# What layers 2 and 3 make of the context alone, moved into the first six steps of layer 0 and kept in DRAM

## The chip, the cores and the metric

The kernel runs on one core of one Trainium2 chip. TensorE (PE) multiplies, VectorE (DVE), ScalarE (ACT) and GpSimd (POOL) work on what it leaves in PSUM and on SBUF, and SyncE (SP) only issues DMAs. Every engine takes its instructions in the order of the program and waits on semaphores for the others. Time is the device time of one launch in microseconds; a comparison goes by the median of several runs.

## The reference, cut to what matters

Four layers follow each other on `x` (4 batches, 1024 rows, 256 features); each also reads the same context `ctx` (4 batches, 77 rows, 256 features), with 16 heads.

```
x = L0(x, ctx)   # causal self-attention joined with the context's keys, then a feed-forward net
x = L1(x, ctx)   # Taylor-feature attention on the context, and a window of 64 on x itself
# L2: cross-attention, heads of 16
q = x @ Wq.T + bq;  k = ctx @ Wk.T + bk;  v = ctx @ Wv.T + bv
p = softmax(where(mask, -inf, (q k^T / 4) * fside))
x = layernorm(x + (p v) @ Wo.T + bo)
# L3: cross-attention, heads of 64
n = rmsnorm(x)
p = softmax((n @ wq) (ctx @ wk)^T)
x = x + (p (ctx @ wv)) @ wo
```

In layers 2 and 3, `k`, `v`, every product of `v` with its head's rows of `Wo` or `wo`, and in layer 3 the product of `k` with its head's rows of `wq`, depend on the context and the weights alone, not on `x`.

## The kernel before, in words

**Layer 0 and layer 1.** Each batch is worked in four *quads* of four heads. A step of layer 0 (`step`, L449) takes the maxima of one quad (`Max0`: scores on PE, `tensor_reduce` into `mpart` on DVE, L565) paired with the weights of the quad before (`Sum0`: scores again, `exp` on ACT, L630, then the product with the values). Both write pairs of PSUM banks out of a pool of two (`big`). After each such burst comes a gap (`gap`, L419), where jobs are advanced: a `Job(gen, n, a, b)` (L400) is to have made n of its steps in proportion to the share of the step that has passed between a and b. What the jobs make is filler for PE: projections of the next quad, statistics, the feed-forward net of the batch before (`ffn`, L764). All fillers share a PSUM pool of three banks, `sm`. Step (b, quad) = (0, 0) has no weights beside the maxima. The order within an engine is the order in which the program is written out; nothing is reordered later.

**Layers 2 and 3** work tile by tile (128 rows of `x`, 32 tiles) in *slots* (`slot2` L1217, `slot3` L1362), software-pipelined over three or four tiles, with jobs in two gaps of each slot. `jobs2` and `jobs3` (L1569, L1581) give the jobs of a batch. What depends on the context alone is made for one batch during the batch before:

- In layer 2, `prep2(b)` (L1176) makes the values and keys (`apart2`, L1131: `pk` on PE, bias on DVE, one copy for each of four heads with the others masked, on POOL), then `U` = each head's values times its rows of `Wo` (`folded_values`, L1153), then the features and the queries of the batch. For batch 0 it runs alone, between the layers (L1551).
- `folded_values` makes 16 heads in 8 steps; a step has two matmuls (`pu`), an eviction on ACT and one on DVE (`us`, four buffers) and about three DMAs that put the 77 rows of each head where `U` wants them: `U` is a list of 16 x 77 = 1232 rows in chunks of 128.
- In layer 3, `folded3(b)` (L1320) makes the keys (`pk`), `G` = keys times `wq` (`pg`), the values (`pk`) and `U`. A slot then multiplies `x`'s features with `G` (`ps<-G,xT`) and the softmax with `U` (`po<-U,pT`).

**Queues.** All DMAs are issued by SP, in the order of the program: at the start the loads, then for each quad the spreading of its queries and keys to their rows (`spread`, L331; a stage buffer `st` to `qk`), in layer 2 two loads for each tile (`load_sides`, L1209), in layer 3 the output.

**SBUF.** The weights live in slots with tags: `s3` holds `w1`, later layer 2's weights; `s4` holds `w2`, later layer 3's `wq`; `s7` holds layer 1's `wout`; `hT` (3 buffers) and `y` belong to the feed-forward net. `first.close()` (L1544) gives the memory of layers 0 and 1 to the pool `late`.

Of the kernel before, what the change touches and what calls it, by code (L numbers as in the profile page):

```python
# [31 lines left out]
def tile_xattn_seq(ctx: ExitStack, tc: tile.TileContext, d: dict, out: bass.AP):  # L32
# [123 lines left out]
    for b in range(1, NB):  # L156
        load_x(b)
    ctn = work.tile([S, NB - 1, D], F32, name="ctn", tag="hT", bufs=3)
    nc.sync.dma_start(out=ctn, in_=d["ctx_1024"][1:NB].rearrange("b s e -> s b e"))

    def other_contexts():
# [8 lines left out]
    w1 = wpool.tile([P, 2, FF], F32, name="w1", tag="s3")  # L170
    load_plain(w1, d["L0_xattn_w1"])
    w2 = wpool.tile([P, 8, D], F32, name="w2", tag="s4")
    load_plain(w2, d["L0_xattn_w2"])
    load_cols_of(
        ("L0_xattn_gf", 2), ("L0_xattn_bf", 2), ("L0_xattn_b1", 8), ("L1_xattn_norm_w", 2),
        ("L2_xattn_bq", 2), ("L2_xattn_bk", 2), ("L2_xattn_bv", 2), ("L3_xattn_norm_w", 2),
# [7 lines left out]
    hsel = cpool.tile([P, HH], F32, name="hsel")  # L184
# [23 lines left out]

    def later_constants():
# [18 lines left out]

        nc.gpsimd.memset(hsel, 1.0)
        nc.gpsimd.affine_select(  # L230
            out=hsel, in_=hsel, compare_op=ALU.is_ge, fill=0.0, base=0,
            pattern=[[-DH, HH]], channel_multiplier=1,
        )
        nc.gpsimd.affine_select(
            out=hsel, in_=hsel, compare_op=ALU.is_ge, fill=0.0, base=DH - 1,
            pattern=[[DH, HH]], channel_multiplier=-1,
        )
# [526 lines left out]
    def ffn(b):  # L764
# [5 lines left out]
        for q in range(5):  # L770
            for half in range(2):
                if q < 4:
                    h = hs[q, half] = work.tile([P, 4, D], F32, name="hT", tag="hT", bufs=3)
                    for f in range(4):
                        ph = sm.tile([P, D], F32, name="ph", tag="sm")
                        fs = slice(P * (4 * half + f), P * (4 * half + f + 1))
                        for c in range(2):
                            mm(
                                ph, w1[:, c, fs], yT[:, c, D * q : D * q + D],
                                start=(c == 0), stop=(c == 1),  # L780
                            )
# [8 lines left out]
                if q and half == 0:  # L790
                    h2 = [hs.pop((q - 1, k)) for k in range(2)]
                    for i in range(2):
                        po = sm.tile([P, D], F32, name="po", tag="sm")
                        for f in range(8):
                            mm(
                                po, h2[f // 4][:, f % 4, P * i : P * i + P], w2[:, f, :],
                                start=(f == 0), stop=(f == 7),
                            )
# [6 lines left out]

    l1 = {}
    l1["wout"] = wpool.tile([P, 4, D], F32, name="wout", tag="s7")
    load_plain(l1["wout"], d["L1_xattn_Wout"])
# [306 lines left out]
    l2 = {}  # L1115

    def load2():
        w = wpool.tile([P, 4, 2, D], F32, name="w2s", tag="s3")
        for i, key in enumerate(("L2_Wq_t", "L2_Wk_t", "L2_Wv_t", "L2_Wo_t")):
            l2[key[3:5]] = w[:, i]  # L1120
            load_plain(w[:, i], d[key])
# [4 lines left out]
    def consts2():  # L1126

        l2["hsel"] = late.tile([P, 4], F32, name="hsel4", tag="hsel4", bufs=1)
        nc.gpsimd.tensor_tensor(l2["hsel"], hsel[:, 0:4], hsel[:, 4:8], ALU.add)

    def apart2(b, w, bias):  # L1131


        pk = sm.tile([P, 2, S], F32, name="pk2", tag="sm")
        for o in range(2):
            for c in range(2):
                mm(
                    pk[:, o, :], w[:, c, P * o : P * o + P], ctxT[:, b, c, :],
                    start=(c == 0), stop=(c == 1),
                )  # L1140
        kp = late.tile([P, 2, S], F32, name="kp", tag="kp", bufs=1)
        kb = late.tile([P, 2, 4, S], F32, name="kb", tag="kb", bufs=3)
        for o in range(2):
            nc.vector.tensor_scalar(
                kp[:, o, :], pk[:, o, :], bias[:, o : o + 1], None, ALU.add
            )
            nc.gpsimd.tensor_tensor(
                kb[:, o], kp[:, o, :].unsqueeze(1).to_broadcast([P, 4, S]),
                l2["hsel"].unsqueeze(2).to_broadcast([P, 4, S]), ALU.mult,
            )  # L1150
        return kb

    def folded_values(U, lhs_of, rhs_of, head_of):  # L1153


        for f in range(8):
            us = late.tile([P, 2, D], F32, name="us", tag="us", bufs=4)
            pu = [sm.tile([P, D], F32, name="pu", tag="sm") for _ in range(2)]
            for e in range(2):
                mm(pu[e][:S], lhs_of(f, e), rhs_of(f, e), skip_group_check=True)  # L1160
            nc.scalar.copy(us[:S, 0, :], pu[0][:S])
            nc.vector.tensor_copy(us[:S, 1, :], pu[1][:S])
            for e in range(2):
                at = S * head_of(f, e)
                done = 0
                while done < S:
                    c, p0 = divmod(at + done, P)
                    n = min(P - p0, S - done)
                    nc.sync.dma_start(out=U[p0 : p0 + n, c, :], in_=us[done : done + n, e, :])
                    done += n  # L1170
            yield
# [4 lines left out]
    def prep2(b):  # L1176

        x = xs[b]
        vb = apart2(b, l2["Wv"], cols["L2_xattn_bv"])
        yield  # L1180
        kb = apart2(b, l2["Wk"], cols["L2_xattn_bk"])
        yield
        U = late.tile([P, NC, D], F32, name="U2", tag="qu")

        yield from folded_values(
            U, lambda f, e: vb[half_rows(e), f // 4, f % 4, :],
            lambda f, e: l2["Wo"][half_rows(e), f // 4, :],
# [5 lines left out]
        for o in range(2):  # L1193
            for q in range(2):
# [10 lines left out]
                if o and q:  # L1205
                    shared["b2", b] = (qT, kb, U)
# [416 lines left out]
```

## Time and profile before

| what | value |
|---|---|
| median of 3 runs | 2560.67 us (2560.18 to 2564.87) |
| the profiled execution, its own time | 2567.04 us |
| its span, first to last instruction | 2565.3 us |
| mean granted TensorE clock | 0.965 |
| busy: PE, PE weight loads | 2351.2 us (92%), 1432.8 us (56%) |
| busy: DVE, ACT, POOL | 1444.1 us (56%), 1025.3 us (40%), 605.5 us (24%) |
| layer 0's first step begins | 41.2 us |
| layers 0 and 1 end | about 1825 us |
| layer 2's slots | about 1850 to 2194 us |
| layer 3's slots | about 2190 to 2562 us |

A row of the windows view has the stretch, its length, the busy time and the number of instructions for PE, PEld, DVE, ACT and POOL, the granted TensorE clock, the share of the DMA engines and GB/s. A row of the groups view has the line, engine, operation, tiles out<-in, shapes, the number of instructions, then busy time and mean duration of one in ns, then the idle time of that engine just before them. One fp32 matmul stands as two records on PE, and matmuls overlap: busy time divided by the count is what one record costs in a stream, the mean is its latency. L45 is the helper that issues nearly all matmuls, so groups are told apart by their tiles.

### The profile page before, as it was taken

To read this page: it belongs to the slowest core of one execution; us is meant where nothing else is said; L and a number is where in the kernel's file an instruction comes from. 1 tells how busy PE (TensorE), PEld (TensorE's weight loads), DVE (VectorE), ACT (ScalarE), POOL (GpSimd) and SP (SyncE) were. 2 spreads that over 40 slices of the span, in tenths; PEclk is the share of its full clock that TensorE was granted. 3 is DMA by queue.
4 is the path that set the end of the run, shared out by engine and by line. 5 is a ranking of instruction groups with operands and counts; after the bars stand their busy time and mean duration, and the time that the engine had idled before them with its cause. 6 is when DMAs were issued, how large, how long until landed. Compare 5 with 4: busy or idle time off the path is not lost.

```text
span 2565.3 us, 40942 instructions
## 1 busy us (share of the span) xinstructions
PE 2351.2 (92%) x16658; PEld 1432.8 (56%) x16658; DVE 1444.1 (56%) x2429; ACT 1025.3 (40%) x1700; POOL 605.5 (24%) x867
## 2 busy tenths in 40 slices
PE   5888788989989898999999999999798998999999
PEld 3333333444444443445567666666476776777877
DVE  4645566544664446542644444444388898675554
ACT  1234343433433443444334434345365655232222
POOL 2011131111301113101422323333133333212212
PEclk8899998999999999999899999999899999999999
DMA  5000000000000001000100211011232321001000
GB/s 152 14 14 5 14 6 14 6 14 2 5 14 6 14 6 34 1 9 10 18 7 12 57 18 18 15 17 39 74 119 85 104 75 58 14 23 31 15 29 17
DMA packets 55631, 75.86 MB, mean 30 GB/s; under 512 B 14823, under 2 KB 46483, under 8 KB 55443
## 3 DMA queue, kind: packets, MB, share of 16 engines
q1 hardware_dynamic: 55442, 73.24, 11.2%
q8 instruction: 132, 2.16, 0.4%
q14 instruction: 57, 0.46, 0.1%
HBM read 41.30 MB, written 4.19 MB: 18 GB/s over the span
## 4 chain that ended last, share of the span: by engine, by line
PE 75%; DVE 14%; ACT 5%; issue 3%; DMA 1%; POOL 1%; SPq 1%; DVEq 0%; ACTq 0%; POOLq 0%
PE ps L45 32%; PE po L45 15%; DVE mpart L565 6%; PE pp L45 5%; PE pv L45 5%; PE ph L45 4%; ACT pe L630 2%; PE psT L1106 2%; PE ppv L45 2%; PE pvw L45 2%; PE pk L45 2%; PE pu L45 1%; PE pvl L45 1%; PE ptx L302 1%; PE pt L506 1%
## 5 line engine op out<-in xcount | busy, mean ns | idle before, releaser
L45 PE MATMUL ps<-qk 32*128 32x192 f32 (+8 forms) x5760 | 631.4, 473 | 130.4 <-DVE mpart L565 69.9
L630 ACT ACTIVATE pe<-ps 128x1024 f32<-128x1024 f32 (+2 forms) x384 | 363.2, 952 | 673.0 <-PE ps L45 667.1
L565 DVE TENSOR_REDUCE mpart<-ps 128x2 f32<-128x1024 f32 (+3 forms) x448 | 409.3, 933 | 361.6 <-PE ps L45 360.7
L45 PEld LDWEIGHTS ps<-qk 32*128 32x128 f32 (+1 forms) x5760 | 295.5, 187 | 420.6 <-DVE mpart L565 166.3
L45 PE MATMUL po<-U,pT 128*128 128x256 f32 (+1 forms) x1280 | 295.3, 386 | 3.2 <-DVE x L1270 2.9
L45 PEld LDWEIGHTS po<-U,pT 128*128 128x128 f32 (+1 forms) x1280 | 242.0, 193 | 48.3 <-issue 12.7
L633 POOL TENSOR_SCALAR_AFFINE_SELECT pe<-pe 128x256 f32<-128x256 f32 (+1 forms) x192 | 94.8, 494 | 613.7 <-ACT pe L630 602.4
L877 DVE TENSOR_REDUCE mrow<-ps 128x4 f32<-128x768 f32 x128 | 122.6, 958 | 144.7 <-PE ps L45 144.3
L1107 ACT COPY pT<-psT 128x512 f32<-128x512 f32 (+1 forms) x192 | 92.8, 519 | 248.9 <-PE psT L1106 248.5
L952 ACT ACTIVATE pew<-ps 128x768 f32<-128x768 f32 x128 | 103.5, 812 | 175.2 <-PE ps L45 174.4
L957 POOL TENSOR_SCALAR_AFFINE_SELECT pew<-pew 128x512 f32<-128x512 f32 x128 | 81.3, 635 | 349.2 <-ACT pew L952 349.0
L45 PE MATMUL pv<-pe,va 128*32 128x512 f32 (+3 forms) x1536 | 163.6, 514 | 0.1
L45 PE MATMUL ps<-G,xT 128*128 128x308 f32 x512 | 143.0, 423 | 0.0
L1401 POOL TENSOR_TENSOR s<-s,den 128x1232 f32<-128x1232 f32 x32 | 71.9, 2248 | 278.9 <-DVE den L1400 268.5
L45 PE MATMUL ph<-yT,w 128*128 128x256 f32 x512 | 136.0, 400 | 0.9 <-DVE qk L491 0.9
L1232 ACT ACTIVATE s<-s,nm 128x77 f32<-128x77 f32 x512 | 131.2, 348 | 11.3 <-DVE nm L1264 11.3
L45 PEld LDWEIGHTS ph<-yT,w 128*128 128x128 f32 x512 | 92.4, 195 | 50.9 <-issue 37.7
L45 PE MATMUL po<-w,hT 128*128 128x256 f32 x512 | 118.0, 384 | 0.0
L1106 PE MATMUL psT<-ident,s 128*128 128x128 f32 x640 | 93.9, 277 | 24.0 <-POOL s L1278 9.7
L45 PEld LDWEIGHTS po<-w,hT 128*128 128x128 f32 x512 | 96.1, 191 | 21.7 <-issue 9.5
L45 PEld LDWEIGHTS ps<-G,xT 128*128 128x128 f32 x512 | 92.5, 190 | 26.9
L491 DVE TENSOR_TENSOR qk<-pm,qk 128x512 f32<-128x512 f32 x64 | 44.1, 689 | 106.4 <-PE pm L489 106.4
(180 smaller groups left out, 3246.9 us busy)
## 6 DMA issues: line engine op xcount, KB each, us to landing
side<-in_fside_t SPq DMA_DIRECT2D x32, 616.0 KB
qk<-st SPq DMA_DIRECT2D x256, 64.0 KB
side<-in_mask_t SPq DMA_DIRECT2D x32, 154.0 KB
U<-us SPq DMA_DIRECT2D x56, 77.0 KB
x<-in_x SPq DMA_DIRECT2D x8, 512.0 KB
out<-x SPq DMA_DIRECT2D x32, 128.0 KB
w<-in_L_xattn_w SPq DMA_DIRECT2D x2, 1024.0 KB
qk<-kc SPq DMA_DIRECT2D x64, 4.8 KB
```

The lines of the kernel that those rows point to most:

```text
L45: nc.tensor.matmul(o, lhsT, rhs, start=start, stop=stop, **kw)
L491: nc.vector.tensor_tensor(qs, pm.rearrange("p i n -> p (i n)"), qs, ALU.add)
L565: nc.vector.tensor_reduce(mpart[bl][:, i, 2 * p : 2 * p + 2, ci], ps[:, :, o : o + w], axis=AX.X, op=ALU.max,)
L630: nc.scalar.activation(pp[:n, :, o:512], ps[:n, :, o:512], AF.Exp, scale=SC)
L633: nc.gpsimd.affine_select(out=own, in_=own, compare_op=ALU.is_ge, fill=0.0, base=0, pattern=[[0, 2], [0, k], [1, P]], channel_multiplier=-1,)
L877: nc.vector.tensor_reduce(mo, ps.rearrange("p j (i n) -> p j i n", i=2)[:, :, :, 0 : P + WIN], axis=AX.X, op=ALU.max, negate=True,)
L952: nc.scalar.activation(pp[:, :, :, 0 : P + WIN], ps.rearrange("p j (i n) -> p j i n", i=2)[:, :, :, 0 : P + WIN], AF.Exp, scale=SC,)
L957: nc.gpsimd.affine_select(out=pf[:, :, 0:P], in_=pf[:, :, 0:P], compare_op=ALU.is_ge, fill=0.0, base=0, pattern=[[0, 4], [1, P]], channel_ ...
L1106: nc.tensor.transpose(ps[:, k, :], s[:, P * c : P * c + P], ident)
L1107: nc.scalar.copy(pT[:, 4 * group : 4 * group + n, :], ps[:, 0:n, :])
L1232: nc.scalar.activation(hs, hs, AF.Exp, bias=p1["nm"][:, h : h + 1], scale=SC)
L1401: nc.gpsimd.tensor_tensor(s3, s3, den.unsqueeze(2).to_broadcast([P, H, S]), ALU.mult)
```

## The change

For all four batches at once (4 x 77 = 308 columns, `NS`), layer 0's first six steps make what layers 2 and 3 need of the context: in step (0, 0) layer 2's values (`values2`), `U` (`folded2`) and keys (`keys2`), in (0, 1) layer 3's keys (`heads3("wk")`), in (0, 2) its `G` (`keys3`), in (0, 3) its values (`heads3("wv")`), in (1, 0) and (1, 1) its `U` (`folded3`). The finished tiles go through one staging tile `stg` of 1024 columns, in which `place(n, size)` hands out n regions in turn, and are written to DRAM (`kept_k`, `kept_u`, `kept_g`). `folded` takes 128 of the 308 rows at a time, whatever batch they are of, so a head needs three matmuls where it needed four. Layer 2's keys come back in one load for all batches, `U` and `G` by batch, at 0.4 of the batch before; `G` comes in runs of 77 values.

The weights for this are loaded at the start, in `s3`, `s4` and `y`; the feed-forward net's `w1` and `w2`, and `wout`, come later, when these slots are free. The masks of heads are made ahead of layer 0 (`head_masks`, which POOL and DVE run behind the first constants), and the contexts of batches 1 to 3 are turned at the start of step (0, 0). `apart2`, `folded_values`, `consts2` and the old `folded3` are gone.

```diff
     ctn = work.tile([S, NB - 1, D], F32, name="ctn", tag="hT", bufs=3)
     nc.sync.dma_start(out=ctn, in_=d["ctx_1024"][1:NB].rearrange("b s e -> s b e"))
+    load_cols_of(("L2_xattn_bv", 2), ("L2_xattn_bk", 2))
+    l2 = {}
+    w2s = wpool.tile([P, 3, 2, D], F32, name="w2s", tag="s3")
+    for i, key in enumerate(("L2_Wv_t", "L2_Wo_t", "L2_Wk_t")):
+        l2[key[3:5]] = w2s[:, i]
+        load_plain(w2s[:, i], d[key])
+    load_x(1)
+    l3 = {}
+    def load3(key, pool, tag, **kw):
+        l3[key] = pool.tile([P, 2 if key in ("wk", "wv") else 8, 1024 if key in ("wk", "wv") else D],
+                            F32, name="l3" + key, tag=tag, **kw)
+        load_plain(l3[key], d["L3_" + key])
...
+    load3("wk", wpool, "s4")
+    for b in range(2, NB):
+        load_x(b)
+    load3("wq", work, "y", bufs=1)
...
+    def head_masks():
...
+        nc.vector.tensor_reduce(
+            hsel2, hsel.rearrange("p (r e) -> p e r", e=2), axis=AX.X, op=ALU.add
+        )
+        nc.vector.tensor_reduce(
+            hsel4, hsel.rearrange("p (g e) -> p e g", e=4), axis=AX.X, op=ALU.add
+        )
...
+    NS = NB * S
+    dram = ctx.enter_context(tc.tile_pool(name="dram", bufs=1, space=bass.MemoryType.DRAM))
+    kept_k = dram.tile([P, 2, 4, NS], F32, name="kept_k")
+    kept_g = dram.tile([P, 2, 8, 2, NS], F32, name="kept_g")
+    kept_u = [dram.tile([NB, H, S, D], F32, name=f"kept_u{i}") for i in range(2)]
+    stg = wpool.tile([P, 1024], F32, name="stg", tag="s7")
+    turn = [0]
...
+    def place(n, size):
+        turn[0] += 1
+        o = 1024 // n * (turn[0] % n)
+        return stg[:, o : o + size]
...
+    def of_contexts(w, o):
+        pk = sm.tile([P, NB, S], F32, name="pk", tag="sm")
+        for c in range(2):
+            mm(pk, w[:, c, P * o : P * o + P], ctxT[:, :, c, :], start=(c == 0), stop=(c == 1))
+        return pk.rearrange("p b s -> p (b s)")
+    def values2():
+        vb = shared["v2"] = []
+        for o in range(2):
+            pk = of_contexts(l2["Wv"], o)
+            v = work.tile([P, 2, NS], F32, name="v2", tag="hT", bufs=3)
+            for e in range(2):
+                nc.vector.tensor_scalar(
+                    v[:, e, :], pk, cols["L2_xattn_bv"][:, o : o + 1], hsel2[:, e : e + 1],
+                    ALU.add, ALU.mult,
+                )
+            vb.append(v)
+            yield
...
+    def keys2():
+        for o in range(2):
+            pk = of_contexts(l2["Wk"], o)
+            for e in range(4):
+                k = place(3, NS)
+                nc.vector.tensor_scalar(
+                    k, pk, cols["L2_xattn_bk"][:, o : o + 1], hsel4[:, e : e + 1],
+                    ALU.add, ALU.mult,
+                )
+                nc.sync.dma_start(out=kept_k[:, o, e, :], in_=k)
+                if e % 2:
+                    yield
...
+    def folded(dst, pairs, act):
+        for heads, lhs, rhs in pairs:
+            for at, lo in ((0, 0), (P, P), (NS - P, 2 * P)):
+                hi = at + P
+                us = place(2, 512).rearrange("p (e n) -> p e n", e=2)
+                pu = [sm.tile([P, D], F32, name="pu", tag="sm") for _ in range(2)]
+                for e in range(2):
+                    mm(pu[e], lhs[e][:, at:hi], rhs[e], skip_group_check=True)
+                for e in range(2):
+                    evict(us[:, e, :], pu[e], act or e == 0)
+                b = lo // S
+                while lo < hi:
+                    n = min(hi, S * b + S) - lo
+                    nc.sync.dma_start(
+                        out=dst[b, heads, lo - S * b : lo - S * b + n, :].rearrange("e s n -> s e n"),
+                        in_=us[lo - at : lo - at + n],
+                    )
+                    lo, b = lo + n, b + 1
+                yield
...
+    def folded2():
...
+                for e in range(2):
+                    h = HH * o + 2 * r + e
+                    two = [slice(HP * (r + k), HP * (r + k) + HP) for k in range(2)]
+                    pairs.append((
+                        slice(h, h + 3, 2), [shared["v2"][o][q, e, :] for q in two],
+                        [l2["Wo"][q, o, :] for q in two],
+                    ))
...
+    def heads3(key):
+        kv = shared[key] = [
+            work.tile([P, 3, NS], F32, name="kv3", tag="hT", bufs=3) for _ in range(3)
+        ]
+        for f in range(8):
+            evict(kv[f // 3][:, f % 3, :], of_contexts(l3[key], f), f % 2)
+            yield
...
+    def keys3():
+        for f in range(8):
+            for c in range(2):
+                pg = [sm.tile([P, NS], F32, name="pg", tag="sm") for _ in range(2)]
+                for e in range(2):
+                    r = slice(64 * e, 64 * e + 64)
+                    mm(
+                        pg[e], l3["wq"][r, f, P * c : P * c + P], shared["wk"][f // 3][r, f % 3, :],
+                        skip_group_check=True,
+                    )
+                for e in range(2):
+                    g = place(3, NS)
+                    evict(g, pg[e], e == 0)
+                    nc.sync.dma_start(out=kept_g[:, c, f, e, :], in_=g)
+                yield
...
+    def folded3():
+        two = [slice(0, 64), slice(64, P)]
+        yield from folded(
+            kept_u[1],
+            [
+                (slice(2 * f, 2 * f + 2), [shared["wv"][f // 3][r, f % 3, :] for r in two],
+                 [l3["wo"][r, f, :] for r in two])
+                for f in range(8)
+            ],
+            False,
+        )
...
+    def load_folded(i, b):
+        U = late.tile([P, NC, D], F32, name=f"U{i + 2}", tag="qu")
+        rows_of_u = kept_u[i][b].rearrange("h s n -> (h s) n")
+        n = P * (NC - 1)
+        nc.sync.dma_start(
+            out=U[:, 0 : NC - 1, :], in_=rows_of_u[0:n].rearrange("(c p) n -> p c n", p=P)
+        )
+        nc.sync.dma_start(out=U[0:HSIZE, NC - 1, :], in_=rows_of_u[n:HK])
+        return U
+    def loads2(b):
+        shared["u2", b] = load_folded(0, b)
+        yield
...
     def prep2(b):
         x = xs[b]
-        vb = apart2(b, l2["Wv"], cols["L2_xattn_bv"])
-        yield
-        kb = apart2(b, l2["Wk"], cols["L2_xattn_bk"])
-        yield
-        U = late.tile([P, NC, D], F32, name="U2", tag="qu")
-        yield from folded_values(
-            U, lambda f, e: vb[half_rows(e), f // 4, f % 4, :],
-            lambda f, e: l2["Wo"][half_rows(e), f // 4, :],
-            lambda f, e: 8 * (f // 4) + 4 * e + f % 4,
-        )
...
             a = tiles[i] = dict(b=b, t=t)
-            qT, kb, _ = shared["b2", b]
...
-                        kb[r, o].rearrange("p h s -> p (h s)"),
+                        ps[:, e, 0 : 4 * S].rearrange("p (h s) -> p h s", s=S),
+                        qT[r, o, P * t : P * t + P],
+                        kb[r, o, :, b, :],
                     )
...
+    def loads3(b):
         G = late.tile([P, 2, 8, 2, S], F32, name="G3", tag="gs")
-        for g in range(2):
-            for c in range(2):
-                pg = [sm.tile([P, 4, S], F32, name="pg3", tag="sm") for _ in range(2)]
...
-                        )
-                for e in range(2):
-                    nc.scalar.copy(G[:, c, 4 * g : 4 * g + 4, e, :], pg[e])
-                yield
-        vT = yield from heads("wv")
-        U = late.tile([P, NC, D], F32, name="U3", tag="qu")
-        yield from folded_values(
-            U, lambda f, e: vT[half_rows(e), f, :], lambda f, e: l3["wo"][half_rows(e), f, :],
-            lambda f, e: 2 * f + e,
+        nc.sync.dma_start(
+            out=G.rearrange("p c f e s -> p (c f e) s"),
+            in_=kept_g.rearrange("p c f e (b s) -> p (c f e) b s", s=S)[:, :, b, :],
         )
-        shared["b3", b] = (G.rearrange("p c f e s -> p c (f e s)"), U)
...
             j.append(Job(keep("c00", None), 1, 0.1, 0.2))
             j.append(Job(values0(0, 0), 4, 0.2, 0.8))
-            j.append(Job(other_contexts(), 3, 0.5, 0.9))
+            j.append(Job(other_contexts(), 3, 0.0, 0.1))
             j.append(Job(feature_weights(), 3, 0.5, 1.0))
+            j.append(Job(values2(), 2, 0.1, 0.2))
+            j.append(Job(folded2(), 24, 0.2, 1.0))
+            j.append(Job(keys2(), 4, 0.5, 0.9))
+        if (b, quad) == (0, 1):
+            j.append(Job(heads3("wk"), 8, 0.0, 1.0))
+        if (b, quad) == (0, 2):
+            j.append(Job(keys3(), 16, 0.0, 1.0))
+        if (b, quad) == (0, 3):
+            j.append(Job(heads3("wv"), 8, 0.0, 1.0))
+        if (b, quad) in ((1, 0), (1, 1)):
+            j.append(Job(keep("f3", folded3), 15 - 6 * quad, 0.0, 1.0, quad == 1))
         if quad == 0 and b + 1 < NB:
             j.append(Job(stats0(b + 1), 8, 0.3 if b == 0 else 0.0, 1.0))
...
         for quad in range(4):
+            if (b, quad) == (0, 1):
+                load3("wo", wpool, "s3")
+            if (b, quad) == (0, 2):
+                load3("wv", wpool, "s4")
+            if (b, quad) == (1, 0):
+                load_w2()
+            if (b, quad) == (1, 2):
+                load_w1()
+                load_wout()
...
-    l3["wo"] = late.tile([P, 8, D], F32, name="l3wo", tag="wo", bufs=1)
-    load_plain(l3["wo"], d["L3_wo"])
-    consts2()
+    kb = shared["k2"] = late.tile([P, 2, 4, NB, S], F32, name="kb", tag="kb", bufs=1)
+    nc.sync.dma_start(out=kb.rearrange("p o h b s -> p o h (b s)"), in_=kept_k)
     load_sides(0)
+    run(loads2(0))
...
-            j.append(Job(prep2(b + 1), 18, 0.1, 0.95, True))
+            j.append(Job(loads2(b + 1), 1, 0.4, 0.41))
+            j.append(Job(prep2(b + 1), 12, 0.1, 0.95, True))
...
         return j
...
+            j.append(Job(loads3(b + 1), 1, 0.4, 0.41))
         return j
```

## The prediction

> **What bounds the kernel now.** I read the busy shares first (PE 92%, the next engine 56%), then the chain that ended last, whose shares are three quarters PE; then PE's busy time stage by stage, since a stage decides what a matmul is worth in it. Numbers are us unless they say otherwise. The first rows are five steps of layer 0, (0, 0), (0, 3), (1, 1), (2, 1) and (3, 3), each from the last maxima of the step before to its own (`mrow`, L573); then come the second and fourth batch of layer 2 and the second and fourth of layer 3.
>
> ```profile
> PE 75%; DVE 14%; ACT 5%; issue 3%; DMA 1%; POOL 1%; SPq 1%; DVEq 0%; ACTq 0%; POOLq 0%
> ```
>
> ```profile
> 41.20:86.80 45.60, 39.76 (x182) 21.52 (x184) 32.14 (x56) 0.00 (x0) 0.00 (x0) 0.69 0.14 22
> ...
> 209.40:274.20 64.80, 56.79 (x432) 24.96 (x433) 30.66 (x44) 26.42 (x30) 7.29 (x14) 1.00 0.03 5
> ...
> 336.60:397.80 61.20, 54.02 (x422) 22.88 (x422) 41.28 (x79) 26.47 (x31) 20.88 (x32) 1.00 0.04 6
> ...
> 632.20:702.70 70.50, 64.45 (x468) 31.32 (x468) 43.86 (x84) 31.12 (x35) 22.31 (x34) 1.00 0.03 5
> ...
> 1073.90:1147.30 73.40, 67.47 (x482) 33.57 (x482) 34.56 (x50) 30.47 (x34) 9.60 (x17) 1.00 0.03 5
> ```
>
> ```profile
> 2093.00:2178.00 85.00, 77.01 (x452) 61.84 (x451) 77.63 (x128) 48.83 (x170) 29.73 (x30) 0.94 0.22 71
> ...
> 1919.90:2007.80 87.90, 78.21 (x399) 58.89 (x397) 74.25 (x112) 48.77 (x167) 29.52 (x30) 0.94 0.27 87
> ...
> 2282.90:2381.60 98.70, 97.28 (x546) 77.42 (x545) 55.79 (x94) 29.28 (x52) 20.89 (x20) 1.00 0.08 24
> 2480.30:2556.70 76.40, 76.32 (x376) 62.70 (x374) 38.54 (x53) 22.32 (x33) 18.53 (x15) 1.00 0.04 14
> ```
>
> Layer 3 is PE and nothing else (97.28 of 98.70): a matmul taken away is its busy time saved. Layer 2 has PE at 89 to 91% and DVE at 84 to 91%; neither alone sets the time. The steps of layer 0 have 12% idle on PE, but it is latency between PE and DVE: step (2, 1) does the work of (1, 1) and some feed-forward besides, 10.43 more of PE, and takes 9.3 longer (0.89); (3, 3) against (0, 3) has 10.68 more and takes 8.6 longer (0.81). So filler costs **0.85 of its busy time** there. In the first step ACT is idle throughout, the clock is 0.69.
>
> **What is removed.** These rows give busy time for all four batches, and, with the two after them, the price of a record.
>
> ```profile
> L45 PE MATMUL pu<-w2s,kb 64*77 64x256 f32 x128 | 35.1, 501 | 8.2 <-ACT us L1161 3.0 <-POOL kb L1147 2.7 <-DVE kp L1144 2.1
> ...
> L45 PE MATMUL pg<-kv,l3wq 64*128 64x77 f32 x256 | 19.0, 278 | 1.0 <-ACT G L1352 0.9
> ...
> L45 PE MATMUL pu<-l3wo,kv 64*77 64x256 f32 x128 | 26.3, 406 | 1.7 <-DVE xT L308 1.3 <-ACT us L1161 0.3
> ...
> L45 PE MATMUL ps<-G,xT 128*128 128x308 f32 x512 | 143.0, 423 | 0.0
> ...
> L45 PE MATMUL ps<-kb,qT 64*128 64x308 f32 x256 | 50.4, 473 | 0.0
> ```
>
> With the three `pk` groups (15.5, 15.5 and layer 2's 8.6) that is 120.0 of PE, 30 a batch.
> - *Layer 3*, batches 0 to 2 each carry the next one's `folded3`: in the stretch 2381.6 to 2480.3, `pk` 3.8 + 3.8, `pg` 4.7, `pu` 6.3 = 18.6. Three times 18.6 = 56, all on the path; batch 0 also has DVE busy 68 of its 89, so I take **-54**.
> - *Layer 2's slots.* Three batches lose (35.1 + 8.6) / 4 = 10.9 of PE each, the last 18.6: 51 in all. DVE loses its half of `us` (0.414 x 8) and, in three, `kp` (0.29 x 4): 3 x 4.5 + 3.3 = 17. Were DVE the bound, -17; were PE, 0.85 x 51 = -43. Both engines are near full, DVE where the normalisation runs, PE elsewhere: **-25**, a little nearer DVE's end.
> - *Between the layers* `prep2(0)` runs alone:
>
> ```profile
> 1824.37 1.97 PEld L45 LDWEIGHTS pk<-ctxT,w2s 128*128 128x128 f32 x16
> ...
> 1828.36 20.33 SPq L1169 DMA_DIRECT2D U<-us  x25
> ...
> 1834.80 0.37 ACT L1161 COPY us<-pu 77x256 f32<-77x256 f32 x1 [1.86 <-DMA U<-us]
> ...
> 1838.55 1.12 PE L302 MATMUL ptx<-ident,x 128*128 128x128 f32 x4
> ```
>
> The features begin at 1838.55; they could at 1825.5, when the last `x` is added: **-13**. The keys, `U` and side must then come in by 1836.5 instead of 1849.7. Issued from 1822 on (when the memory comes free), 1.26 MB of keys and 0.77 MB of side take 7 at the 316 GB/s of the first loads: about 1831 with 2 of landing. `U` is wanted three slots later. Hidden, with 5 to spare.
> POOL's `kb` (10.9) and 200 DMA issues of SP also go, off the path. **Removed: 54 + 25 + 13 = 92.**
>
> **What is added.** Full-width matmuls over 308 columns cost 143.0 / 512 = 0.279 a record, 64-row pairs 50.4 / 256 = 0.197, `pu` 26.3 / 128 = 0.206.
> - Steps (0, 1) and (0, 3): 8 x 2 matmuls = 32 records, 8.9 each. (0, 2): 32 matmuls, 64 records, 12.6. (1, 0) and (1, 1): 48 matmuls, 96 records, 19.8. Together 50.2, at 0.85 **+43**. Evictions: 4 on DVE in a step of `heads3`, 16 in `keys3`, 24 over the two of `folded3`, at 0.41 to 0.47; the feed-forward that gave the 0.85 has as many for its matmuls. DMA waits: the steps of these jobs are 4 apart, two or three regions, so a landing has 8 us and is hidden; if not, DVE and ACT stop with it and each step gives some 2 us.
> - Step (0, 0): values and keys 16 records (4.5) and `folded2` 96 records (19.8): 24 of PE at full clock, against 39.76 x 0.69 = 27 there now. PE alone would want 51, more than 45.6. But the pace is set by `stg`. A step of `folded2` evicts twice on ACT (0.37 each) and issues two DMAs on average (0.6 to 0.8 each; 20.33 / 25 in the row above). The chain of that stretch has a DMA at 2.0 to 2.3 from issue to landing. So a region comes free after 0.7 + 0.7 + 2.1 = 3.5, two regions give a step each 1.8: 24 x 1.8 = 43 over what was 36 (shares 0.2 to 1.0). `keys2` uses three regions that overlap the two, so each of its four turns waits for the last `U` to land and then holds up the next: 3.5 + 2.5, of which some 1.5 lies beside matmuls: 4 x 4.5 = 18. The evictions of `keys2` are DVE's; behind them are the maxima, and PE waits for these. 9 + 43 + 18 = 70: **+25**. Ends: +12 (waits hidden, clock recovers) and +50 (each step waits for its own DMA: 24 x 3.6).
> - The start: the two mask reductions of DVE stand behind POOL's constants (free at 22.1), and behind them `kc` and `xn`, which began at 13.0 and 15.2. I make the projections 3.6 later; but the queue with the loads holds the spreading to 38.7 while it is ready at 33.8, so what stays is the queue: 0.25 MB and two issues more, **+1** (0 to 5).
> - Reading back: `U` and `G` come in some 45 us ahead. *A rule against it*: the Trainium skill, "DMA: Bandwidth & Descriptors", Specifications, wants 512 B or more for line rate; `G`'s runs are 308 B, and no row has a load of such runs from DRAM. At the rate of the first loads 1.26 MB take 4; by the rule, at half rate say, 8. Either fits before a batch of layer 3; once, in the last batch of layer 2, it stands ahead of a tile's side: 0 or +4. I take 0.
>
> *A second rule*: "TensorE: Matmul & The Clock Gate", table "Why this matters", warns that PE gaps over some 3 us bring the half clock. Layer 2 loses filler and its clock is 0.94 already (2093 to 2178). If the lost 0.06 became 0.12: 340 us x 0.06 = +20. But layer 3's last batch, with least filler, has 1.00, and the idle of layer 2 is 10 of 88 in short waits. By the row 0, which I take.
>
> **Sum**: -92 + 43 + 25 + 1 = -23. Against the profiled execution: 2567.0 - 23 = 2544. That one stands 6.4 above the median, so the median goes from 2560.67 to **2538**.
>
> **Rivals.**
> - *Layer 0 swallows it.* PE idles 5.8 of the first step and 7 to 13 of each of the next five. At 0.5 instead of 0.85, +25, and the first step +12: -92 + 25 + 12 + 1 = -54, 2507. For it: ACT idle, a clock that more work could lift. Against it: 0.81 and 0.89.
> - *The first step becomes a DMA loop* (other sign): if the two regions act as one, because `keys2` overlaps both or SP's issues lag, 24 steps x 3.6 and the turns of `keys2` make it 9 + 86 + 18 = 113, +67: -92 + 43 + 67 + 1 = +19, 2580. It decides from +48 on: (93.6 - 9 - 18) / 24 = 2.8 for a step. For it: the eviction that waits 1.86 for a DMA, with four buffers. Against it: each of those steps issued three DMAs.
> - *The read-back is late*: `G` and `U` come 10 late at three batches and at layer 2's start: 2538 + 40 = 2578, no gain. Against it: 45 us of lead and DMA engines 90% idle in layer 3.
>
> **How the numbers follow.** Main case 0.52 (2518 to 2555), swallowed 0.2, DMA loop 0.2, late 0.08. The range leaves out the outer halves of the outer cases: 2502 to 2576. A change under 0.2%, 5 us, is about what a measurement of this kernel can't tell from none. Faster: 0.49 + 0.2 + 0.03 = 0.72; same 0.02 + 0.03 + 0.02 = 0.07; slower 0.21.
>
> **What would show it.** Step (0, 0) from 45.6 to about 70, with ACT's evictions and `keys2` waiting on DMAs to `kept_u`; the next five steps longer by 6 to 11 each; features straight behind layer 1's last addition; layer 3's batches at about 80 instead of 98.7, and no wait for `G`, `U` or the keys. A first step beyond 95, or layer 2's batches still at 85, makes the prediction wrong.

## The result and the profile after

| | before | after |
|---|---|---|
| median of 4 runs | 2562.66 us (2560.18 to 2564.87) | **2538.57 us** (2531.39 to 2543.16) |
| ratio, with its 95% interval | 1 | 0.9904 (0.9875 to 0.9932) |
| profiled execution, its own time and span | 2567.04, 2565.3 us | 2535.56, 2533.8 us |
| mean granted clock | 0.965 | 0.963 |
| busy PE, DVE, ACT | 2351.2, 1444.1, 1025.3 us | 2305.5, 1446.8, 1019.8 us |

The change makes the kernel 1.0% faster, and the forecast of 2538 stands beside 2538.57. So close an agreement is luck: one term of the sum was 19 us off, and other differences made up for it.

The chain that ended last, by engine, in the kernel after; DMA has 2% of it where it had 1%.

```profile
PE 75%; DVE 13%; ACT 5%; DMA 2%; issue 2%; POOL 1%; SPq 1%; ACTq 0%; DVEq 0%; POOLq 0%
```

The windows of the kernel after, in the columns of before. The first row is step (0, 0), the second and third are (0, 3) and (1, 1), the fourth is all that lies between layers 1 and 2. Then come the second and the fourth batch of layer 2, and the second of layer 3.

```profile
40.20:130.20 90.00, 66.04 (x294) 39.05 (x293) 38.48 (x68) 18.00 (x49) 0.00 (x0) 0.66 0.30 76
...
274.20:343.70 69.50, 64.99 (x464) 30.30 (x464) 32.62 (x48) 28.09 (x35) 7.37 (x14) 1.00 0.08 19
...
416.00:480.90 64.90, 59.67 (x456) 25.49 (x456) 44.83 (x88) 29.13 (x39) 20.98 (x32) 1.00 0.17 45
1893.40:1906.20 12.80, 12.80 (x58) 6.78 (x57) 6.00 (x8) 2.75 (x4) 0.00 (x0) 1.00 0.77 283
1969.10:2045.10 76.00, 68.02 (x347) 50.88 (x345) 71.01 (x101) 46.24 (x158) 26.81 (x26) 0.98 0.31 100
2121.30:2202.00 80.70, 60.51 (x302) 46.49 (x299) 74.08 (x120) 42.47 (x149) 28.98 (x29) 0.92 0.31 91
...
2289.40:2367.00 77.60, 77.60 (x381) 63.51 (x381) 54.08 (x85) 21.97 (x32) 20.87 (x20) 1.00 0.17 47
```

The first row is where the time was spent: 90.0 where there were 45.6, with PE idle for 24.0 of it. The last is where it was won: 98.7 became 77.6, PE busy without a gap. In the fourth batch of layer 2 PE lost 16.5 of its busy time, and the batch only 3.3 up to the first maxima of layer 3; DVE is busy 74.08 of the 80.7 shown, which makes it the likely limit there (no run tests it). In the second, 10.2 less of PE brought 11.9.

Both profiles can be cut at the same events (first maxima, last `mrow` of a step, last addition to `x`, first row maxima `nm` of layer 2, first maxima of layer 3), and then every microsecond has a place:

| stretch | before | after | difference | forecast |
|---|---|---|---|---|
| up to the first maxima | 41.2 | 40.2 | -1.0 | +1 |
| step (0, 0) | 45.6 | 90.0 | **+44.4** | **+25** |
| steps (0, 1) to (1, 1) | 311.0 | 350.7 | +39.7 | +43 |
| rest of layer 0 | 749.5 | 744.6 | -4.9 | 0 |
| layer 1 | 677.5 | 667.9 | -9.6 | 0 |
| between layers 1 and 2 | 28.7 | 12.8 | -15.9 | -13 |
| layer 2 | 336.9 | 309.2 | -27.7 | -25 |
| layer 3 to the end | 374.9 | 318.4 | -56.5 | -54 |
| sum | 2565.3 | 2533.8 | -31.5 | -23 |

Step (0, 0) of the kernel after, its waits (engine, line, what it waited for: us in total, times, longest):

```profile
PEld pu L45 <- ACT stg L858: 25.6, 17, 4.4
ACT stg L858 <- DMA kept_k<-stg: 25.5, 6, 7.4
...
ACT stg L858 <- DMA kept_u<-stg: 22.2, 9, 9.9
...
PE pu L45 <- ACT stg L858: 16.1, 14, 3.7
DVE stg L889 <- DMA kept_u<-stg: 16.0, 3, 7.9
```

PE waits for ACT's evictions, and ACT for a region of `stg`: 25.5 for the keys' transfers, 22.2 for those of `U`; DVE, which evicts the keys, waits another 16.0 for `U`. Pieces of the chain that ended last in that step (start us, us, what):

```profile
54.50 4.35 DMA kept_u<-stg
...
90.26 2.36 DMA kept_u<-stg
...
93.73 3.70 DMA kept_u<-stg
...
97.71 0.61 DVE stg L889
98.34 1.83 DMA kept_k<-stg
...
101.43 2.49 DMA kept_u<-stg
...
105.02 3.70 DMA kept_u<-stg
```

A landing takes 1.83, 2.4 or 3.7 (once 4.35), by which transfer it is. 1.83 belongs to the keys: 128 rows of one piece of 1.2 KB. By the kernel's row ranges, a step's 128 rows of `U` are cut at the batches into 77 and 51, or 26, 77 and 25 (and a last one of 52). The ones on the chain at 3.7 and 4.35 are the 51 rows of two pieces of 1 KB, the ones at 2.4 the 25 rows.

### The profile page after: what moved, and what is told of

Same layout as the page of the kernel before. It is cut to its first block, busy times and chain, and to the rows that moved or that the text cites. A ratio compares the mean times of both kernels' runs of the same rounds, so it can differ in the third digit from the quotient of the medians.

```text
span 2533.8 us, 39765 instructions
## 1 busy us (share of the span) xinstructions
PE 2305.5 (91%) x16162; PEld 1387.2 (55%) x16162; DVE 1446.8 (57%) x2411; ACT 1019.8 (40%) x1684; POOL 593.9 (23%) x850
## 4 chain that ended last, share of the span: by engine, by line
PE 75%; DVE 13%; ACT 5%; DMA 2%; issue 2%; POOL 1%; SPq 1%; ACTq 0%; DVEq 0%; POOLq 0%
PE ps L45 32%; PE po L45 15%; PE pp L45 6%; PE pv L45 5%; DVE mpart L599 5%; PE ph L45 4%; PE ppv L45 2%; PE psT L1276 2%; PE pvw L45 2%; ACT pe L664 2%; DVE s L1373 2%; DMA kept_u<-stg 1%; PE ptx L336 1%; PE pvl L45 1%; PE pk L45 1%
## 5 line engine op out<-in xcount | busy, mean ns | idle before, releaser
L45 PE MATMUL ps<-qk 32*128 32x192 f32 (+8 forms) x5760 | 620.2, 471 | 102.3 <-DVE mpart L599 54.8
L45 PE MATMUL po<-U,pT 128*128 128x256 f32 (+1 forms) x1280 | 295.6, 387 | 15.8 <-DVE x L1395 14.2
```

The lines of the kernel that those rows point to most:

```text
L45: nc.tensor.matmul(o, lhsT, rhs, start=start, stop=stop, **kw)
```

## The experiments

**Layer 3's half alone.** Only what layer 3 needs is made ahead; layer 2 makes its own keys and `U` in its slots as before.

```diff
-            j.append(Job(values2(), 2, 0.1, 0.2))
-            j.append(Job(folded2(), 24, 0.2, 1.0))
-            j.append(Job(keys2(), 4, 0.5, 0.9))
...
-            j.append(Job(loads2(b + 1), 1, 0.4, 0.41))
-            j.append(Job(prep2(b + 1), 12, 0.1, 0.95, True))
+            j.append(Job(prep2(b + 1), 18, 0.1, 0.95, True))
```

> Layer 3's half of the change alone; layer 2 makes its keys, values and U by batch as before. Step (0, 0) should be back at 45 to 47 us and layer 2 at its old 28.7 us of start and 66, 88 and 85 us for the first three batches; the steps (0, 1) to (1, 1) stay about 40 us longer, layer 3 about 56 us shorter. Theory (by the changed kernel's trace layer 2's half costs 44 in step (0, 0) and brings 16 + 24): 2535 us, no slower than the whole change. Rival (by the prediction's sum layer 2's half costs 25 and brings 13 and about 18): 2545 us.

Measured: 2535.01 (2526.52 to 2538.62), ratio 0.989 (0.986 to 0.992), as the theory said. The interval leaves the rival's 2545 out. Half of the change gives as much as the whole: step (0, 0) takes 43.7, the steps (0, 1) to (1, 1) 348.4, and layer 3 takes 316.6, near the 318.4 of the whole change. The row of step (0, 0):

```profile
41.20:84.90 43.70, 37.40 (x187) 20.49 (x186) 32.16 (x57) 2.89 (x3) 0.00 (x0) 0.75 0.21 47
```

**Layer 2's half alone.** Layer 3 folds its keys and values in its own slots as before. (Its last two blocks of `wo` stand in a tile of their own.)

```diff
-        if (b, quad) == (0, 1):
-            j.append(Job(heads3("wk"), 8, 0.0, 1.0))
-        if (b, quad) == (0, 2):
-            j.append(Job(keys3(), 16, 0.0, 1.0))
...
```

> Layer 2's half of the change alone; layer 3 makes its keys, G, values and U by batch as before. Step (0, 0) about 90 us, steps (0, 1) to (1, 1) at their old 61 to 65 us, layer 3 at its old 98.7 us a batch, layer 2's start 13 us instead of 29. Theory: +44 - 16 - 24 makes 2566 us, not faster than before. Rival (prediction's sum): +25 - 13 - 18 makes 2556 us.

Measured: 2564.00 (2557.98 to 2572.68) over 12 runs, ratio 1.0019 (1.0002 to 1.0037). Its windows: step (0, 0), layer 2, layer 3.

```profile
40.70:131.00 90.30, 65.94 (x294) 39.41 (x296) 38.46 (x69) 18.10 (x49) 0.00 (x0) 0.66 0.29 75
1875.70:2188.80 313.10, 280.28 (x1474) 214.97 (x1473) 277.66 (x398) 186.83 (x640) 107.00 (x105) 0.95 0.29 93
2188.80:2563.10 374.30, 366.89 (x1993) 293.17 (x1991) 221.55 (x364) 109.46 (x188) 83.11 (x77) 1.00 0.07 22
```

Layer 2 wins 23.8 here and the stretch before it 15.9. Step (0, 0) takes the same 90 as in the whole change and costs 44.7. So this half comes out at nothing or a little slower, and the cost of its first step alone decides that.

**Keys beside `U`, not in it.** `keys2` gets four places of its own, and `U` keeps its two regions.

```diff
+        own = work.tile([P, 4, 512], F32, name="own", tag="pe")
...
-                k = place(3, NS)
+                k = own[:, e, 0:NS]
```

> The whole change, but the keys of layer 2 are staged in places of their own, so that they never wait for a DMA of U; U keeps its two places. Theory: the four turns of the keys go, step (0, 0) about 70 us, total about 2519 us. Rival (the two places of U and the queue set the pace alone): 83 us or more, total 2532 us or more.

Measured: 2532.79 (2529.92 to 2536.52), ratio 0.9884 (0.9854 to 0.9915); step (0, 0) in 77.0, between the two expectations.

```profile
40.30:117.30 77.00, 62.33 (x295) 37.32 (x296) 38.58 (x69) 18.23 (x49) 0.00 (x0) 0.71 0.36 89
```

```profile
ACT stg L858 <- DMA kept_u<-stg: 28.9, 12, 10.1
```

The windows row shows the step, and the line of its waits what is left: no wait for `kept_k`, 28.9 for `kept_u`. The overlap of the keys with the two regions cost 13 in this step, and `U` with two regions costs more than the forecast gave it. The medians don't show the 13: the two ratios' intervals overlap, and in this profile the rest of layer 0 took 758 instead of 745.

**One transfer for a step of `U`.** The rows of a step go to DRAM in one DMA of 128 (or 52) rows, in another order; the kernel leaves out putting them back, so it serves for its times alone.

```diff
-                b = lo // S
-                while lo < hi:
...
+                nc.sync.dma_start(
+                    out=dst.rearrange("b h s n -> (b h s) n").rearrange("(h r) n -> h r n", r=NS)[
+                        heads, lo:hi, :
+                    ].rearrange("e s n -> s e n"),
+                    in_=us[lo - at : P],
+                )
```

> The whole change with its two places, but each step of layer 2's and layer 3's U is written to DRAM by one DMA of 128 rows (52 in every third step) instead of two, three or one by batch; the same bytes go to the same tensor in another order of rows, so U is read back with its rows permuted and the output is not the reference's. Theory (a part of 51 rows lands only 3.7 us after its issue, whole tiles after about 2): DMA pieces of the chain at about 2 us, step (0, 0) from 90 to about 75 us, total about 2523 us. Rival (any write to DRAM takes 3.7 us behind the others, the count of DMAs is no matter): step (0, 0) stays at 85 us or more.

Measured in one run: 2528.3; step (0, 0) in 78.6. The steps (0, 1) to (1, 1) take 342.5 instead of 350.7. Of these 8, step (1, 0), which writes `U` of layer 3 in the same way, has 6.5 (65.8 instead of 72.3; 70.7 to 72.3 in all seven kernels that write it in parts), and its evictions' waits for `kept_u` fall from 9.1 to 3.0. Its row of step (0, 0), then pieces of the chain of that step:

```profile
40.80:119.40 78.60, 64.49 (x294) 37.85 (x296) 38.60 (x69) 18.32 (x49) 0.00 (x0) 0.68 0.31 88
```

```profile
72.95 2.46 DMA kept_u<-stg
80.37 1.92 DMA kept_u<-stg
83.04 1.80 DMA kept_k<-stg
107.72 2.13 DMA kept_u<-stg
```

No landing on the chain is above 2.5, and in the share by lines `kept_u` falls from 31.9 to 8.1%. So the cuts at the batches cost 11: some of the pieces land later, and SP issues two or three instead of one.

The run changes both the number of transfers and the rows of each, but the traces can tell them apart. They keep every rise of the semaphore that tells a landing (in the trace files, not in a view shown here). Apart from a first rise at the issue, which 128 rows don't have, it rises 16 times for 128 rows, 11 for 77, 13 for 26 and 52, 5 for 25, and 3 for 51, in every transfer of step (0, 0). From issue to landing 77 rows take 2.36 in the median and the smaller 51 rows 3.78. The kernel before shows the same in layers 2 and 3, where `U<-us` went in parts of nearly equal size (medians of eight): 51 rows with 3 rises 2.87, 52 rows with 13 rises 2.10, 53 rows with 1 rise 4.70, 54 rows with 9 rises 2.40. So it is the row count that makes a part late, not its size or the number of parts.

**More places for `U`.** `folded2` takes eight places in two tiles, in the slots of layer 0's `pe`, which step (0, 0) does not use; `stg` is left to the keys.

```diff
+    def half_places():
+        wide = [work.tile([P, 4, 512], F32, name="wide", tag="pe") for _ in range(2)]
+        return [w[:, j, :] for w in wide for j in range(4)]
...
-                us = place(2, 512).rearrange("p (e n) -> p e n", e=2)
+                us = places[0] if places else place(2, 512)
+                if places:
+                    places.append(places.pop(0))
...
-        yield from folded(kept_u[0], pairs, True)
+        yield from folded(kept_u[0], pairs, True, half_places())
```

> The whole change, but U of layer 2 is staged in eight places (two tiles that nothing else uses in that step) instead of two; the keys have the old staging tile to themselves. Theory (the first step is paced by places that wait for their DMAs): step (0, 0) falls from 90 to 60 to 65 us, set by 51 us of TensorE at full clock and its waits, total about 2511 us. Rival (TensorE at half clock and its three filler banks pace it): still over 80 us, total 2530 us or more.

Measured: 2521.24 (2518.43 to 2522.64), ratio 0.984 (0.9816 to 0.9864); step (0, 0) in 70.3. The direction is the theory's; the step is 5 longer than the upper end it gave. Its windows row, then what remains of DMA in its chain:

```profile
40.70:111.00 70.30, 62.95 (x294) 36.44 (x293) 38.39 (x68) 18.13 (x49) 0.00 (x0) 0.70 0.38 97
```

```profile
80.95 4.19 DMA kept_k<-stg
86.06 4.00 DMA kept_k<-stg
```

PE is idle for 7.4 instead of 24.0. The three regions of the keys are now what is waited for, and the keys' landing on the chain has grown from 1.8 to 4.0 and 4.2.

**Three trials after that.** The first splits the evictions of `U` between ACT and DVE, with the eight places. The second gives `U` six places (one tile and the two regions of `stg`) and the keys six of their own. The third is the second with the split. The first diff is against the kernel with eight places, the second against the kernel after.

```diff
-        yield from folded(kept_u[0], pairs, True, half_places())
+        yield from folded(kept_u[0], pairs, False, half_places())
```

> Eight places for layer 2's U as before, and its two evictions a step go one to ScalarE and one to VectorE instead of both to ScalarE. Theory (with the DMA wait gone, TensorE and ScalarE wait for each other over three banks): step (0, 0) from 70 to about 63 us, total about 2514 us. Rival (VectorE's maxima come later by as much): 70 us or more, 2521 us.

```diff
+        own = work.tile([P, 4, 512], F32, name="own", tag="pe").rearrange("p j n -> p (j n)")
+        turn2 = 0
...
-                k = place(3, NS)
+                k = own[:, NS * turn2 : NS * turn2 + NS]
+                turn2 = (turn2 + 1) % 6
...
+        wide = work.tile([P, 4, 512], F32, name="wide", tag="pe")
+        return [wide[:, j, :] for j in range(4)] + [stg[:, 0:512], stg[:, 512:1024]]
```

> Six places for layer 2's U and six others for its keys, all evictions of U on ScalarE. Theory (two waits of 4 us for the keys' DMA stand in the chain of the step with eight places): step (0, 0) from 70 to about 62 us, total about 2513 us. Rival (the waits lie beside the matmuls of U): 68 to 71 us, 2519 us or more.

> Both at once: six places for layer 2's U, six for its keys, and U's evictions split between ScalarE and VectorE. Theory (what is left in the first step is TensorE waiting for evictions, as the split showed no more than 1 us where the keys' DMA still stood in the chain): step (0, 0) from 64 to about 60 us, total about 2505 us. Rival (VectorE's maxima wait behind the evictions): 64 us or more, 2509 us or more.

| version | median us | ratio, interval | step (0, 0) |
|---|---|---|---|
| after | 2538.57 | 0.9904 (0.9875 to 0.9932) | 90.0 |
| evictions split, eight places | 2513.32 | 0.9849 (0.9799 to 0.9899) | 69.3 |
| **six places for `U`, six for the keys** | **2509.00** | **0.9821 (0.9783 to 0.9858)** | **64.1** |
| the same, evictions split | 2517.85 | 0.9870 (0.9838 to 0.9901) | 70.1 |

The ratios are to runs of the kernel before made beside each version, so they compare better than the medians. The rows of step (0, 0), with six and six places and then with the split:

```profile
40.90:105.00 64.10, 56.82 (x294) 34.54 (x293) 38.11 (x68) 17.76 (x49) 0.00 (x0) 0.75 0.42 107
```

```profile
40.70:110.80 70.10, 62.55 (x299) 36.86 (x298) 47.09 (x91) 11.82 (x27) 0.00 (x0) 0.70 0.38 98
```

Splitting the evictions does not help: against the version without it, the step is 1 shorter in the first pair, where the ratios are equal, and 6 longer in the second. DVE is busy longer in both (47.09 instead of 38.11 in the second). But the 6 lie in PE's busy time, 62.55 instead of 56.82 at a clock of 0.70 instead of 0.75, while PE's idle time is 7.6 and 7.3. So the second pair does not show that DVE's maxima stand behind the evictions.

The same holds for the 6 between eight places and six and six. PE's idle time is 7.4 and 7.3, its busy time 62.95 and 56.82, the clock 0.70 and 0.75, and the ratios' intervals overlap (0.9816 to 0.9864, 0.9783 to 0.9858). The keys' transfers leave the chain of the step, but that their places bring anything beyond the clock is not shown. With six and six ACT waits 5.4 for staging in the whole step, in three waits:

```profile
ACT wide L858 <- DMA kept_k<-own: 2.4, 1, 2.4
ACT wide L858 <- DMA kept_u<-wide: 2.3, 1, 2.3
ACT wide L858 <- DMA kept_u<-stg: 0.7, 1, 0.7
```

This version takes 1.8% off the kernel before, nearly twice what the change does, with the same work; PE is busy 56.82 of its 64.1, so most of what is left there is PE's own at the clock that it gets.

**The kernel before once more**, for the stretches that the change doesn't touch.

> The kernel before, profiled a second time. In its first profile layer 1 took 677.5 us, in those of all five kernels with the change or a part of it 667 to 671 us. Theory (layer 1 is untouched; the 10 us were TensorE at half clock in that one execution): 667 to 671 us here too. Rival (the change helps layer 1, by its loads of weights that are gone): 677 us again.

Measured: 2562.53, span 2560.8. Layer 1 took 668.1 and the rest of layer 0 756.7. Layer 1 by windows, in the first profile of before, in this one, and in the kernel after, a fence each:

```profile
1147.30:1824.80 677.50, 657.62 (x6013) 419.73 (x6013) 300.27 (x593) 285.57 (x370) 210.75 (x337) 0.97 0.10 21
```

```profile
1152.30:1820.40 668.10, 647.05 (x6013) 414.36 (x6013) 299.75 (x593) 285.58 (x370) 210.96 (x337) 0.99 0.11 21
```

```profile
1225.50:1893.40 667.90, 647.25 (x6013) 413.12 (x6014) 299.89 (x593) 285.57 (x370) 210.75 (x338) 0.99 0.09 16
```

The same 6013 matmuls, at a clock of 0.97 or 0.99: the 9.6 that layer 1 seems to have won are the first profile's, not the change's. The rest of layer 0 lies between 742 and 758 in all eleven profiles and its -4.9 means as little.

## Why the prediction was right, and where it was not

*Layer 3, -54: right.* -56.5, and the mechanism is the one given. Cut at each batch's first maxima, the batches lose 14.8, 20.5, 20.4 and 0.7, where the sum had 18.6 for each of three; in the second PE is busy for the whole 77.60, and the first has DVE busy 68.42 of 74.0, the brake that the prediction named.

*Layer 2, -25: right.* -27.7, by batch -3.5, -11.9, -9.0 and -3.3, between the two bounds of -17 and -43. The first and the last won about what DVE lost (3.9 and 3.6), though PE lost 8.0 and 16.5 there; the second won about what PE lost (10.2), against 3.2 of DVE. The first batch before and after, a fence each:

```profile
1853.50:1919.90 66.40, 60.67 (x305) 44.48 (x304) 59.31 (x76) 45.44 (x158) 22.71 (x24) 0.92 0.36 115
```

```profile
1906.20:1969.10 62.90, 52.70 (x261) 39.06 (x260) 55.41 (x63) 42.95 (x150) 19.92 (x19) 0.92 0.37 121
```

*Between the layers, -13: right, a little small.* -15.9. The features start with the last addition to `x` (1893.2 and 1893.4), and the keys' load is issued 2.6 ahead of that addition (3.5 in the prediction). No engine waits for `kb` or `U` there.

*Steps (0, 1) to (1, 1), +43: right in sum.* +39.7, by step +8.9, +12.5, +4.7, +9.9 and +3.7, so three of the five lie outside the 6 to 11 named. The added groups in the kernel after are 56.5 of PE (11.2 and 10.1 of `pk`, 15.8 of `pg`, 19.4 of `pu`), not 50.2, at a granted clock of 0.94 in these steps where it was 0.98; so filler cost 0.70 of its busy time rather than 0.85, and the two errors met, which is luck. The rival "layer 0 swallows it" (0.5) is out. *One of its reasons was wrong*: "a landing has 8 us and is hidden". It is not quite: evictions wait 9.1 for `kept_u` in step (1, 0), and one transfer for a step of `U` made that step 6.5 shorter.

*Step (0, 0), +25: wrong in size.* It came to +44.4, within the ends of +12 and +50 and 3.6 short of the +48 from which the rival with the other sign decides. The prediction's own terms were 9 of other work, 24 x 1.8 of `U` and 18 of keys. With the keys apart the step is 77.0, so the keys' part was 13 (forecast 18), and each step of `U` cost (77.0 - 9) / 24 = 2.8, not 1.8. The 1.8 for a step of `U` is the term that was mis-sized, and it failed at two places:
- *The landing.* It was taken as 2.1 from the chain's `U<-us`; on the chain after it is 2.4 to 4.4. The part that is late is the 51 rows of a step's second transfer, though the 77 rows ahead of it are more. The Trainium skill, "DMA: Bandwidth & Descriptors", section "Why a DMA increments its semaphore by 16 and not by 1", gives the rule that fits: a DMA takes the largest number of engines, up to 16, that divides its rows. By it 128 rows go to 16 engines, 77 to 11, 51 to 3, 25 to 5, and the semaphores' rises are these numbers. The trace before already had late parts of 51 and 53 rows (2.87 and 4.70); the prediction read the landings of its chain alone.
- *SP's queue.* The prediction counted issues of `U` and left out what else stands in that queue. Between 65.9 and 75.2 SP issues 12 spreads of `qk`, one every 0.63, ahead of the next transfer of `U`; they are 8.6% of the step's chain, 7.8. With the 11 that the cuts cost, that is 19 of the 25 by which `U`'s part was too small; the rest stays open.

What it cost: of the 44.4, PE's idle time is 18.1 (5.8 before, 24.0 after) and its busy time 26.3 (39.76, 66.04). With six and six places the same step takes 64.1, its idle time 7.3 and its busy time 56.82. So the waits for staging cost PE 16.7 of idle time. The other 9.2 between 90.0 and 64.1 are busy time at a clock of 0.66 instead of 0.75; whether the waits lowered the clock, no run shows. "PE alone would want 51" was at full clock; the step had 0.66 to 0.76 in the versions with layer 2's half.

*The start, +1: right but for its sign.* The projections run 3.1 later and the first maxima 1.0 earlier (0.0 against the second profile of before, which has them at 40.2 too); the queue hid the masks as argued.

*Read-back, 0: right, though the transfer is the slower of the two cases.* No engine waits for `G` or `U` anywhere in layers 2 and 3. But the load of `G` is neither free nor at the rate of the first loads. SP's queue at the first batch of layer 3, and the DMA rate in half-microsecond slices from 2138:

```profile
2139.35 0.61 SPq L1441 DMA_DIRECT2D G<-kept_g  x1
2140.00 6.81 SPq L1297 DMA_DIRECT2D U<-kept_u  x1
2146.86 1.32 SPq L1300 DMA_DIRECT2D U<-kept_u  x1
```

```profile
GB/s 0 0 79 128 296 197 384 349 281 280 291 290 256 248 245 249 244 223 82 137 219 207 315 387 379 383 368 362 283 327 412 283 79 5 0 0 0 0 0 0
```

The stretch of `G`'s runs of 308 B goes at 245 to 290 GB/s, `U`'s 1 KB rows at 360 to 390 behind it. The rule of 512 B that the prediction weighed is right in its direction, about 0.7 of the rate instead of the half assumed. While `G` comes in, SP stands 6.81 at the issue of `U` (3.9 to 6.8 over the four batches), and the next side waits behind it; 0 to +4 was the bracket. It came to 0, since no engine waits for that side either (issued at 2148.36, first read at 2153.99).

*The clock, 0: right.* Layer 2 as a whole went from 0.94 to 0.95.

*The sum.* The terms that belong to the change come to -17 (-1.0 + 44.4 + 39.7 - 15.9 - 27.7 - 56.5) where the forecast had -23. The other -14.5 of the two profiles are layer 1 and the rest of layer 0. The medians differ by 24, and how much of that is the clock of single executions is open: the runs of the kernel after alone span 11.8. So the size of the change was forecast about right; that 2538 was met to 1 us was not earned.

## What to carry to other kernels

Work moved into an early stage to free a late one is paid in waits for its staging as much as in matmuls: before adding it, count the places that its results pass through, the transfers of one step, and everything else in the queue that issues them. A place is busy from the eviction to the landing of its *slowest* part, so give two kinds of results places of their own, and cut them by row counts that have a large divisor up to 16 (51 rows landed later than 77, 53 later than 52 or 54). And test the halves of a change alone: here one of them brought everything, and the other paid only after its staging was mended.

## What the runs showed of the hardware that was not expected

**The half clock came without long gaps.** In the version with six and six places no wait of PE in step (0, 0) is over 1.6, yet its clock is 0.75 over the step and 0.50 in two stretches where PE is busy 7.08 and 8.00 of 8.00. The longest wait of PE there, and these stretches:

```profile
PE pu L45 <- DVE own L893: 1.6, 1, 1.6
```

```profile
65.00:73.00 8.00, 7.08 (x29) 4.37 (x24) 3.28 (x4) 1.02 (x3) 0.00 (x0) 0.50 0.51 88
...
81.00:89.00 8.00, 8.00 (x32) 5.11 (x32) 2.87 (x4) 2.08 (x7) 0.00 (x0) 0.50 0.59 170
```

The kernel before has 0.69 in its step. In the kernel after, 99 to 130 us runs at 0.50 throughout. What grants the clock in this step stays open; more PE work in it did not lift it to 1.00 in any version.

**The same transfer landed later behind other transfers.** 128 rows of keys landed in 1.82 to 2.09 in the kernel after and in 4.1 to 4.6 in six of the eight transfers with eight places. The number of places is not the cause: with the keys apart, `U` has its two regions and the keys landed in 4.1 to 4.3. In that run each transfer of keys was issued 0.4 to 1.0 behind one of 51 rows of `U`, and landed 0.4 to 0.9 behind its landing. In the kernel after, the overlapping regions held all but one of the keys' transfers back until `U` had landed. With eight places, the two that landed in 1.83 were issued 2.8 and 3.3 behind the 51 rows. So the order in SP's queue goes with it; by what mechanism was not tested.
